# Values of two cross-attentions in seven block products instead of eight, with the context's sums kept in space that later rows will fill

## The chip, the cores and the metric

The kernel runs on one core of a Trainium2 chip. A core has a matrix engine (TensorE, "PE" in the profile; its weight loads are listed apart as "PEld"), a vector engine (VectorE, "DVE"), an activation engine (ScalarE, "ACT"), a general engine (GpSimd, "POOL") and a queue that issues transfers (SyncE, "SP"). The metric is the device time of one execution in microseconds, the median of several runs.

## What is computed

The reference is a stack of four transformer layers over four batches of 256 rows of 256 numbers, in 32-bit floats. Layer 0 has two cross-attentions to the same context and an MLP; layers 1, 2 and 3 are other attention variants on narrow heads. The change touches only the two attentions of layer 0:

```python
def _cross_attention(q_in, kv_in, wq, bq, wk, bk, wv, bv, wo, bo, bias_k, bias_v):
    qh = (q_in @ wq + bq).reshape(b, q_len, H, K)
    kh = (kv_in @ wk + bk).reshape(b, t, H, K)
    vh = (kv_in @ wv + bv).reshape(b, t, H, K)
    # one learned key and value are appended, then
    weights = softmax(einsum('bqhk,bthk->bhqt', qh, kh) / sqrt(K))
    ctx = einsum('bhqt,bthk->bqhk', weights, vh).reshape(b, q_len, H * K)
    return ctx @ wo + bo
```

Here H is 16 heads of K = 128, kv_in is the context (4 x 256 rows of 256), and wq, wk, wv are 256 x 2048. Queries, keys and values are thus three products of a 1024 x 256 matrix by a 256 x 2048 one, twice.

## The kernel before, in words

Layer 0 loops over two attentions (li), four head groups of four heads (hg) and two pairs of batches (bp): 16 rounds. In each round the queries, keys and values of 4 heads and 512 rows are made, then for each batch of the pair the scores, the softmax, the transposed weights, the weighted values and the projection by wo.

**Seven products for queries and keys.** A product of two matrices of 2 x 2 blocks takes eight block products; Strassen's method in Winograd's form takes seven, at the cost of sums of blocks. The routine seven (line 1029) does this. Its blocks are a 128 x 128 piece of the weights (the stationary operand) and 256 columns of the input. It runs p = 0 and 1 side by side, so it issues 14 products of 256 columns in four tasks on PE, each after the one before: first, second, third, fourth. Between them one PSUM bank, v[0], goes on being added to, while VectorE or ScalarE save its state into a tile u of a ring of three (UU, line 936), and VectorE forms the totals from PSUM and u into the output. The sums of weight blocks are made by GpSimd (sums, line 1015, four subtractions or additions for each head group) and lie in space that the MLP's weights will fill later (place["sq"], place["sk"] in mlp_w0); the sums of inputs are made by VectorE or GpSimd (differences, line 994). The first round's keys are made the plain way.

**Eight products for the values.** In each round the list tV (line 1212) has four tasks on PE. Each multiplies 128 rows of the context (stationary) with 512 columns of wv, in two accumulating products of 128x512; VectorE then adds the bias row bvb into the tile V. bvb is bv less the learned value's bias, and GpSimd subtracts that once for each head group.

**Rows.** rowbc (line 90) holds 3136 numbers of bias and scale rows for all layers, spread to all partitions by one load (all_rows, line 1120, issued as t_rows at line 1148). Layer 0 uses the first 768; the others belong to layers 1 to 3.

**What sets the order.** Nothing is ordered by hand. Each piece is a Task (line 171): an amount of PE time, tasks it must come after, tasks it must be planned behind without waiting for their data, ring buffers it takes and gives back (PSUM banks in the ring PS, V, E, u and so on), and Posts, the work of other engines that follows, each with its cost on every engine that may do it. plan (line 1533) runs a greedy simulation at build time: among the products that can start with least idle time of PE, within 0.2 us (SLACK, line 1524), it takes the one with the highest level, which is the length of the longest chain behind it, corrected by HANDICAPS (line 1648) for each stage and batch. A post goes to the engine that would end it first. Instructions are then issued in that order, and every engine keeps it (Pinned, line 124); the chip's semaphores make them wait for real. A task added anywhere can therefore move later choices.

**What stands around the change.** Weights of a head group live in the ring W0 of two sets (line 917) and are loaded when the group before last is done. t_f0 (line 1408) loads the MLP's weights into mlp_w0 once all queries and keys are made. opened (line 1454) frees layer 0's memory, once its last projections are planned, opens that of the later layers, and only then their weights are loaded. weighted (line 1349) reads V. All instructions carry line 132 in the profile, the helper that records them, so they are told apart by their tiles: wv, wk, wq are weights, ctxT the context, HT the normed input, craw and e the input differences of queries and keys (raw and the first EE tile), f the weight sums, u the saved states, V, qT, kT the results, and ps_pj, ps_s, ps_et, ps_o PSUM banks.

Of the kernel before, what the change touches and what calls it, by code (L numbers as in the profile page):

```python
# [51 lines left out]
def kernel(ctx: ExitStack, tc: tile.TileContext, a: dict, out: bass.AP):  # L52
# [861 lines left out]
    def l0_ring(n, shape, tag):  # L914
        return Ring([l0.tile(shape, F32, tag=f"{tag}{i}", name=f"{tag}{i}") for i in range(n)])
# [5 lines left out]
                for k, shape in (  # L921
                    ("wv", [P, 2, 512]), ("wq", [P, 2, 512]), ("wk", [P, 2, 512]), ("wo", [P, HG, D]),
                    ("bvb", [P, 512]), ("bvl", [P, 512]),
                )
# [5 lines left out]
    for place, f in zip(W0.tiles, mlp_w0):  # L930
        f = f.rearrange("p a b -> p (a b)")
        place["sq"] = f[:, :768].rearrange("p (n q c) -> p n q c", n=3, q=2)
        place["sk"] = f[:, 768:1536].rearrange("p (n q c) -> p n q c", n=3, q=2)
    V0, QT, KT = l0_ring(2, [P, 4, 512], "V"), l0_ring(2, [P, HG, 512], "qT"), l0_ring(2, [P, HG, 2, S + 1], "kT")
    E0, ET, CT = l0_ring(4, [P, HG, S + 1], "E"), l0_ring(3, [P, 2, S], "eT"), l0_ring(2, [P, HG, S], "cT")
# [72 lines left out]
    for bp in range(2):  # L1008
        def block(k, j, bp=bp):
            return ctxT[:, k, (2 * bp + j) * S : (2 * bp + j + 1) * S]  # L1010
# [17 lines left out]

    def seven(b, after, w, key, block, T, to, bias):


        v, u = {}, {}

        def A(p, i, k):
            return w["w"][2]["w" + key][:, k, (2 * p + i) * P : (2 * p + i + 1) * P]

        def sum_(n, p):
            return w["w"][2]["s" + key][:, n, p, :]

# [8 lines left out]

        def saved(n, of, i, gives=()):

            if not bias:
                return [copied(lambda: flat(n), lambda: v[of][2], 512, gives)]
            return [
                affine(
                    lambda p=p: flat(n)[:, p * S : (p + 1) * S], lambda p=p: v[of][2][:, p * S : (p + 1) * S], None,
                    lambda p=p: bias(p, i), gives if p else (),
                )
                for p in range(2)
            ]
# [13 lines left out]
        def second():  # L1073
            for p in range(2):
                product(0, p, sum_(0, p), T[:, 1, :])

        def third():
            for p in range(2):
                product(0, p, A(p, 1, 0), T[:, 0, :])
            for p in range(2):  # L1080
                product(2, p, sum_(1, p), T[:, 2, :], True)

        def fourth():
            for p in range(2):
                product(0, p, sum_(2, p), block(1, 1))
            for p in range(2):
                product(2, p, A(p, 1, 1), T[:, 3, :])

        def last(gives):

            if not bias:
                dst = lambda: to(0)[:, :, 1, :]
                return [copied(dst, lambda: pairs(0), 512, gives)]
# [9 lines left out]
            b, "full", 1.73, first, after, takes=[(PS, v, 0), (PS, v, 1), (UU, u, 0)],  # L1103
            posts=saved(0, 0, 0) + [total(0, 0, 1, 0, [(PS, v, 1), (UU, u, 0)])],
        )
        t2 = Task(b, "full", 0.86, second, [t1], takes=[(UU, u, 1)], posts=saved(1, 0, 1))
        t3 = Task(
            b, "full", 1.73, third, [t2], takes=[(PS, v, 2), (UU, u, 2)],
            posts=saved(2, 0, 1) + [total(1, 1, 2, 2, [(UU, u, 2)])],
        )  # L1110
# [3 lines left out]
        )  # L1114
        made = {}
        for p in range(2):
            made.update({(2 * p, 0): t1, (2 * p + 1, 1): t3, (2 * p, 1): t4, (2 * p + 1, 0): t4})
        return made

    def all_rows(e):  # L1120
        dma.dma_start(rowbc, a["rowvec"].to_broadcast([P, _RB_LEN]))

    finals = [[first_x], [first_x], [second["x"]], [second["x"]]]
    all_qk, all_l0, loads, last_grab, last_e, last_h, t_rows = [], [], [], [], [], [], None
    freed_w, freed_u, freed_e = [], [], []
    for li in range(2):
# [6 lines left out]
        for bp in range(2):  # L1133
# [4 lines left out]
            for b in (2 * bp, 2 * bp + 1):  # L1138
# [8 lines left out]
                if t_rows is None:  # L1147
                    t_rows = load(0, [], "rows", all_rows, 1568, behind=[tn])
                t_plus[b] = plus_row_to(b, [tn, t_rows], lambda b=b: Xb(b), f"L0_xattn_bo{li + 1}")
# [12 lines left out]
        for hg in range(NG):  # L1162
# [36 lines left out]
            for bp in range(2):  # L1199
# [11 lines left out]
                last_grab = [grab]  # L1211
                tV = []
                for i in range(4):
                    v = {}

                    def products(i=i, u=u, v=v, w=w, bp=bp):
                        at_ = (4 * bp + i) * P
                        for k in range(2):
                            pe(v["pt"][2], ctxT[:, k, at_ : at_ + P], w["w"][2]["wv"][:, k, :], k == 0, k == 1)

                    def add(e, i=i, u=u, v=v, w=w):
                        ve.tensor_tensor(u["V"][2][:, i, :], v["pt"][2], w["w"][2]["bvb"], ALU.add)

                    tV.append(
                        Task(
                            b0, "full", 1.71, products, [grab, t_w["wv"], t_w["bv"], t_ctx[b0 + i // 2]],
                            takes=[(PS, v, "pt")], posts=[Post(("DVE",), 605, add, gives=[(PS, v, "pt")])],
                        )
                    )
                made = [{}, {}]  # L1230
                if li == 0 and hg == 0 and bp == 0:
# [25 lines left out]
                for n, key in ((1, "k"), (0, "q")):  # L1257
# [8 lines left out]
                    def bias(p, i, h0=hg * HG, li=li):  # L1266
                        return bqs[li][:, h0 + 2 * p + i : h0 + 2 * p + i + 1]

                    done = seven(
                        b0, [grab, t_S[n], (t_Tq if key == "q" else t_Tk)[bp]], w, key,  # L1270
                        (blocks_q if key == "q" else blocks_k)[bp], (Tq if key == "q" else Tk)(bp), to,
                        bias if key == "q" else None,
                    )
                    made[n].update(done)
                tQ, tK = list(dict.fromkeys(made[0].values())), list(dict.fromkeys(made[1].values()))
# [3 lines left out]
                for bb in range(2):  # L1279
# [46 lines left out]
                    for h in range(HG):  # L1326
# [22 lines left out]
                        def weighted(h=h, x=x, y=y, u=u, bb=bb):  # L1349
                            for kc in range(2):  # L1350
# [6 lines left out]
                            Task(  # L1357
                                b, "full", 0.87, weighted, [t, tV[2 * bb], tV[2 * bb + 1]], behind=tC[:1],
                                takes=[(PS, x, "pt")] + ([(CT, c, "c")] if h == 0 else []),
# [47 lines left out]

    t_f0 = load(0, [t_cols[2]], "f0", run, 2048, (), all_qk)

# [43 lines left out]

    opened = Task(0, None, 0, None, behind=all_l0, posts=[Post(("POOL",), 1500, open_late)])
    opened.fills = [(r, len(r.tiles), len(r.tiles) + n) for r, n, _, _ in later] + [(r, 0, 2) for r in SHIFTS]
# [10 lines left out]
    def run(e):  # L1466
# [8 lines left out]
    t_L = {  # L1475
        k: Task(0, None, 0, None, [opened], posts=[Post(("POOL",), 3500, lambda e, k=k: layers[k].fill())], lag=2.0)
        for k in (1, 2, 3)
# [249 lines left out]
```

## Time and profile before

| What | us |
|---|---|
| median of 3 runs (1383.52 to 1384.44) | 1384.36 |
| the profiled execution | 1383.26 |
| its span, from the first to the last instruction | 1381.5 |
| PE busy within the span | 1333.6 |
| VectorE busy | 783.4 |
| ScalarE busy | 711.1 |
| GpSimd busy | 167.3 |
| last product with wv starts | 695.7 |
| first product of the MLP starts | 728.30 |

The profile is of one execution, so a sum of its rows is made against 1383.26 us; 1.76 us of that lie around the span. An engine's busy time says how much of the span it worked, not whether anyone waited for it. Groups are written out<-in, with partitions x elements; on PE, the part before the shape is rows x columns of the stationary operand. Products overlap in the array, so the distance between the starts of two neighbours says more about their cost than their lengths. Each product of 32-bit floats leaves two records.

### The profile page before, as it was taken

To read this page: it belongs to the slowest core of one execution; us is meant where nothing else is said; L and a number is where in the kernel's file an instruction comes from. 1 tells how busy PE (TensorE), PEld (TensorE's weight loads), DVE (VectorE), ACT (ScalarE), POOL (GpSimd) and SP (SyncE) were. 2 spreads that over 40 slices of the span, in tenths; PEclk is the share of its full clock that TensorE was granted. 3 is DMA by queue.
4 is the path that set the end of the run, shared out by engine and by line. 5 is a ranking of instruction groups with operands and counts; after the bars stand their busy time and mean duration, and the time that the engine had idled before them with its cause. 6 is when DMAs were issued, how large, how long until landed. Compare 5 with 4: busy or idle time off the path is not lost.

```text
span 1381.5 us, 21985 instructions
## 1 busy us (share of the span) xinstructions
PE 1333.6 (97%) x8343; PEld 1009.8 (73%) x8343; DVE 783.4 (57%) x2246; ACT 711.1 (51%) x1728; POOL 167.3 (12%) x283
## 2 busy tenths in 40 slices
PE   5999999999999999999999999999999999999996
PEld 3777787778878787787888867666565667776664
DVE  5655663556656546365542568572665443648886
ACT  2544344454444444344444335527545565889895
POOL 6102020002020200100003411101110002000000
PEclk9999999999999999999999999999999999999999
DMA  7000010100200101000004110000000000000000
GB/s 262 1 32 31 31 47 16 40 22 2 76 16 16 46 31 46 16 32 0 31 1 142 33 47 3 9 1 4 2 5 1 1 2 1 2 9 17 9 4 14
DMA packets 25482, 37.99 MB, mean 27 GB/s; under 512 B 2228, under 2 KB 16070, under 8 KB 25248
## 3 DMA queue, kind: packets, MB, share of 16 engines
q1 hardware_dynamic: 24496, 35.56, 7.9%
q0 software_dynamic: 608, 0.76, 0.5%
q8 instruction: 66, 1.08, 0.3%
q14 instruction: 40, 0.33, 0.1%
q10 hardware_dynamic: 272, 0.26, 0.1%
HBM read 35.52 MB, written 1.05 MB: 26 GB/s over the span
## 4 chain that ended last, share of the span: by engine, by line
PE 87%; DVE 7%; ACT 4%; DMA 1%; issue 1%; POOL 0%; SPq 0%; DVEq 0%; ACTq 0%
PE ps_et L132 24%; PE ps_s L132 22%; PE ps_pj L132 21%; PE ps_o L132 20%; DVE shift L132 2%; ACT eq L132 2%; DVE qk L132 1%; ACT qk L132 1%; DVE eq L132 1%; DMA wv<-in_L_xattn_wv_dram 1%; DVE X L132 0%; ACT e L132 0%; DMA wk<-in_L_xattn_wk_dram 0%; DVE u L132 0%; DVE craw L132 0%
## 5 line engine op out<-in xcount | busy, mean ns | idle before, releaser
L132 ACT ACTIVATE eq<-eq,nm 128x256 f32<-128x256 f32 x256 | 106.2, 509 | 0.0
L132 DVE TENSOR_SCALAR E<-E,rinv 128x257 f32<-128x257 f32 x256 | 84.2, 394 | 2.2
L132 PE MATMUL ps_o<-qk 32*128 32x256 f32 (+1 forms) x318 | 84.9, 459 | 0.3 <-ACT qk L132 0.3
L132 POOL TENSOR_TENSOR X<-X,rowbc 128x256 f32<-128x256 f32 x56 | 41.7, 767 | 340.1 <-DVE e L132 90.3
L132 PE MATMUL ps_et<-qk 32*128 32x256 f32 (+1 forms) x278 | 74.7, 450 | 0.2 <-DVE shift L132 0.2
L132 PE MATMUL ps_s<-qk 32*128 32x256 f32 (+1 forms) x232 | 69.8, 450 | 0.0
L132 PE MATMUL ps_pj<-qk 32*128 32x256 f32 (+1 forms) x196 | 67.1, 487 | 1.0 <-DVE shift L132 1.0
L132 POOL COPY kT<-lks 128x4 f32<-128x4 f32 x32 | 7.2, 236 | 427.5 <-PE ps_o L132 180.7
L132 DVE TENSOR_TENSOR X<-ps_et,X 128x512 f32<-128x512 f32 (+1 forms) x23 | 13.8, 599 | 69.5 <-PE ps_et L132 68.1
L132 PE MATMUL ps_pj<-eq,qk 32*128 32x256 f32 x196 | 50.5, 411 | 1.8 <-DVE qk L132 1.5
L132 PE MATMUL ps_o<-eq,qk 32*128 32x256 f32 x232 | 50.1, 411 | 0.1
L132 DVE TENSOR_REDUCE shift<-ps_o 128x1 f32<-128x512 f32 (+1 forms) x60 | 40.4, 684 | 16.4 <-PE ps_s L132 10.2
L132 PE MATMUL ps_et<-wo,cT 128*128 128x256 f32 x208 | 47.0, 379 | 0.0
L132 PE MATMUL ps_s<-eq,qk 32*128 32x256 f32 x168 | 45.3, 410 | 0.9 <-ACT qk L132 0.9
L132 PEld LDWEIGHTS ps_o<-qk 32*128 32x128 f32 x318 | 39.6, 183 | 7.8 <-issue 2.8
L132 PE MATMUL ps_et<-eq,qk 32*128 32x256 f32 x172 | 43.7, 403 | 0.1
L132 PEld LDWEIGHTS ps_et<-wo,cT 128*128 128x128 f32 x208 | 39.3, 190 | 5.2
L132 DVE TENSOR_REDUCE nm<-ps_pj 128x1 f32<-128x257 f32 x66 | 27.3, 419 | 24.2 <-ACT cT L132 19.5
L132 DVE TENSOR_REDUCE nm<-ps_et 128x1 f32<-128x257 f32 x64 | 26.6, 420 | 24.1 <-ACT cT L132 21.7
L132 DVE TENSOR_TENSOR X<-ps_pj,X 128x256 f32<-128x256 f32 (+1 forms) x13 | 6.9, 527 | 58.2 <-PE ps_pj L132 58.2
L132 PEld LDWEIGHTS ps_et<-qk 32*128 32x128 f32 x278 | 34.6, 183 | 7.2 <-issue 5.2
L132 PE MATMUL ps_s<-eT,V 128*128 128x256 f32 x156 | 39.7, 382 | 0.0
(527 smaller groups left out, 3797.5 us busy)
## 6 DMA issues: line engine op xcount, KB each, us to landing
wk<-in_L_xattn_wk_dram SPq DMA_DIRECT2D x8, 512.0 KB, 3.6
wv<-in_L_xattn_wv_dram SPq DMA_DIRECT2D x8, 512.0 KB, 4.1
wq<-in_L_xattn_wq_dram SPq DMA_DIRECT2D x8, 512.0 KB, 5.3
wo<-in_L_xattn_wo_dram SPq DMA_DIRECT2D x8, 512.0 KB, 4.0
bvb<-in_bv_dram SPq DMA_DIRECT2D x8, 256.0 KB, 5.6
bvl<-in_cols_dram SPq DMA_DIRECT2D x8, 256.0 KB, 5.8
f<-in_L_xattn_w_fc_dram SPq DMA_DIRECT2D x2, 1024.0 KB, 5.1
f<-in_L_xattn_mlp_w_dram SPq DMA_DIRECT2D x2, 1024.0 KB, 5.1
```

Of the source, the lines that this page charges most:

```text
L132: return lambda *args, **more: tc.keep_in_program_order(f(*args, **more))
```

## The change

In every round but the first (li = 0, hg = 0, bp = 0) the values too are made by seven. The parts are:

- **seven** takes its blocks as functions. For values, the stationary blocks are pieces of the context (two halves i of rows, two of columns k, p is the batch of the pair), the moving blocks are 256 columns of wv, and the row bvb is added where the state is saved and at the last step (with_row, VectorE only).
- **Sums of the context** S1 to S4 are made once for each batch (context_sums, on VectorE or GpSimd, 128x128) and stay through both attentions in rowbc, from column 768 on, where the rows of later layers would lie.
- **Sums of wv** are made once for each head group (value_sums, GpSimd, 128x256). One overwrites a block of wv, two lie in the tail of mlp_w0, one in a new tile t4. In the first group they come behind the old value tasks, which read wv.
- **rowbc** is loaded in two parts: its first 768 columns early, the others (rows_of(first_rows, _RB_LEN), 1184 KB) behind all the values. t_f0 is behind all the values too, and opened and the later layers' preparation wait for the second part.
- **weighted** waits for those value tasks that made its heads' half (values_of), of both batches' rows at once.

```diff
-                    ("bvb", [P, 512]), ("bvl", [P, 512]),
+                    ("bvb", [P, 512]), ("bvl", [P, 512]), ("t4", [P, 256]),
...
+        place["tv"] = [f[:, 1536:1792], f[:, 1792:], place["t4"]]
...
-    def seven(b, after, w, key, block, T, to, bias):
+    def seven(b, after, A, sum_, block, T, to, bias, row=None):
...
+        def with_row(dst, of, j, gives=()):
+            def run(e):
+                r = row(j).rearrange("p (o c) -> p o c", o=1).to_broadcast([P, 2, 256])
+                ve.tensor_tensor(dst(), pairs(of), r, ALU.add)
+
+            return [Post(("DVE",), 605, run, gives=gives)]
+
-        def saved(n, of, i, gives=()):
+        def saved(n, of, i, j, gives=()):
+
+            if row:
+                return with_row(lambda: flat(n).rearrange("p (q s) -> p q s", q=2), of, j, gives)
...
         def last(gives):
+            if row:
+                return with_row(lambda: to(0)[:, :, 1, :], 0, 1, gives)
...
-    def all_rows(e):
-        dma.dma_start(rowbc, a["rowvec"].to_broadcast([P, _RB_LEN]))
+    first_rows = _RB["L1_xattn_v_b"][0]
+    SV = rowbc[:, first_rows : first_rows + B * 4 * P].rearrange("p (b n c) -> p b n c", b=B, n=4)
+
+    def rows_of(lo, hi):
+        return lambda e: dma.dma_start(rowbc[:, lo:hi], a["rowvec"][:, lo:hi].to_broadcast([P, hi - lo]))
+
+    def context_sums(b):
+        def run(e):
+            on = ve if e == "DVE" else ge
+
+            def A(i, k):
+                return ctxT[:, k, b * S + i * P : b * S + (i + 1) * P]
+
+            S1, S2, S3, S4 = (SV[:, b, n, :] for n in range(4))
+            on.tensor_tensor(S1, A(1, 0), A(1, 1), ALU.add)
+            on.tensor_tensor(S2, S1, A(0, 0), ALU.subtract)
+            on.tensor_tensor(S3, A(0, 0), A(1, 0), ALU.subtract)
+            on.tensor_tensor(S4, A(0, 1), S2, ALU.subtract)
+
+        return Task(b, None, 0, None, [t_ctx[b]], posts=[Post(("DVE", "POOL"), {"DVE": 840, "POOL": 1600}, run)])
+
+    t_SV = [context_sums(b) for b in range(B)]
+
+    def value_sums(after, behind, w):
+        def run(e):
+            def B_(k, j):
+                return w["w"][2]["wv"][:, k, j * 256 : (j + 1) * 256]
+
+            T2, T3, T4 = w["w"][2]["tv"]
+            ge.tensor_tensor(T3, B_(1, 1), B_(0, 1), ALU.subtract)
+            ge.tensor_tensor(B_(0, 1), B_(0, 1), B_(0, 0), ALU.subtract)
+            ge.tensor_tensor(T2, B_(1, 1), B_(0, 1), ALU.subtract)
+            ge.tensor_tensor(T4, B_(1, 0), T2, ALU.subtract)
+
+        return Task(0, None, 0, None, after, posts=[Post(("POOL",), 2900, run)], behind=behind)
...
-                    t_rows = load(0, [], "rows", all_rows, 1568, behind=[tn])
+                    t_rows = load(0, [], "rows", rows_of(0, first_rows), 384, behind=[tn])
...
+                if li == 0 and hg == 0 and bp == 0:
...
+                    values_of = [[tV[0:2], tV[0:2]], [tV[2:4], tV[2:4]]]
+                    t_TV = value_sums([t_w["wv"]], tV, w)
+                else:
+                    if bp == 0:
+                        t_TV = value_sums([t_w["wv"]], [], w)
...
+                    done = seven(
+                        b0, [grab, t_TV, t_w["bv"], t_SV[b0], t_SV[b0 + 1]], A, lambda n, p, b0=b0: SV[:, b0 + p, n, :],
+                        block, T, to, None, lambda j, w=w: w["w"][2]["bvb"][:, j * 256 : (j + 1) * 256],
                     )
+                    values_of = [[[done[0, j], done[1, j]] for j in range(2)]] * 2
+                    all_v += list(done.values())
...
-                                b, "full", 0.87, weighted, [t, tV[2 * bb], tV[2 * bb + 1]], behind=tC[:1],
+                                b, "full", 0.87, weighted, [t, *values_of[bb][h // 2]], behind=tC[:1],
...
-    t_f0 = load(0, [t_cols[2]], "f0", run, 2048, (), all_qk)
+    t_f0 = load(0, [t_cols[2]], "f0", run, 2048, (), all_qk + all_v)
+    t_rows = load(0, [], "rows", rows_of(first_rows, _RB_LEN), 1184, (), all_v)
...
-    opened = Task(0, None, 0, None, behind=all_l0, posts=[Post(("POOL",), 1500, open_late)])
+    opened = Task(0, None, 0, None, behind=all_l0 + [t_rows], posts=[Post(("POOL",), 1500, open_late)])
```

## The prediction, made before the result was known

> **What bounds the kernel.** I read the engines' busy time first, then stretches of the span, then what TensorE waits for, then single tasks in order of time.
>
> ```profile
> PE 1333.6 (97%) x8343; PEld 1009.8 (73%) x8343; DVE 783.4 (57%) x2246; ACT 711.1 (51%) x1728; POOL 167.3 (12%) x283
> PE 87%; DVE 7%; ACT 4%; DMA 1%; issue 1%; POOL 0%; SPq 0%; DVEq 0%; ACTq 0%
> ```
>
> The first line is the page's busy time, the second the chain that ended last. TensorE (PE) is busy 97% of the span and is 87% of the chain. An average over stages is not enough, so the second view is the busy time by stretch (columns: stretch, length, then busy time of PE, its weight loads, VectorE, ScalarE, GpSimd, each with its count, then granted clock, DMA share, GB/s).
>
> ```profile
> 16.60:60.00 43.40, 40.74 (x160) 27.23 (x160) 31.52 (x84) 21.18 (x63) 21.55 (x32) 1.00 0.27 96
> 100.00:730.00 630.00, 627.45 (x2908) 505.88 (x2907) 340.00 (x849) 279.15 (x803) 59.39 (x101) 1.00 0.09 28
> 730.00:1381.50 651.50, 621.97 (x5089) 441.89 (x5088) 383.83 (x1245) 392.26 (x816) 77.45 (x130) 0.98 0.06 16
> 1200.00:1381.50 181.50, 163.16 (x1572) 115.52 (x1564) 132.82 (x602) 151.57 (x355) 1.42 (x2) 0.98 0.03 10
> ```
>
> The two first attentions, which alone the change touches, end near 728. From 100 to 730 PE idles 630.00 - 627.45 = 2.55 us (0.4%), while VectorE is busy 54% and ScalarE 44%: work taken off PE there is time taken off the span. After 730 PE idles 651.50 - 621.97 = 29.5 us, 18.3 of them in the last 181.5 us. Third view, all that PE waits for between 100 and 730 (total us, times, longest):
>
> ```profile
> PE ps_s L132 <- DVE u L132: 0.7, 3, 0.2
> PE ps_o L132 <- DVE u L132: 0.7, 3, 0.2
> PE ps_pj L132 <- DVE u L132: 0.7, 3, 0.2
> PE ps_et L132 <- ACT eT L132: 0.2, 1, 0.2
> PE ps_et L132 <- DVE u L132: 0.2, 1, 0.2
> ```
>
> Nearly all of it is the u tiles: the queries and keys, already made in seven products, and their handovers.
>
> **What is removed and added on TensorE.** Two kinds of tasks in order of time (start, length, instructions merged):
>
> ```profile
> 85.32 1.03 PE L132 MATMUL ps_et<-ctxT,wk 128*128 128x256 f32 x4
> 86.18 1.03 PE L132 MATMUL ps_s<-craw,f 128*128 128x256 f32 x4
> 87.05 1.03 PE L132 MATMUL ps_o<-e,f 128*128 128x256 f32 x4
> 88.29 1.13 PE L132 MATMUL ps_s<-craw,wq 128*128 128x256 f32 x4 [0.22 <-DVE u L132]
> ...
> 120.88 1.88 PE L132 MATMUL ps_s<-wv,ctxT 128*128 128x512 f32 x4
> 122.60 1.88 PE L132 MATMUL ps_pj<-wv,ctxT 128*128 128x512 f32 x4
> 124.32 1.88 PE L132 MATMUL ps_et<-wv,ctxT 128*128 128x512 f32 x4
> ```
>
> A product of the program leaves two records (the wv groups count 256, and the code has 2 layers x 4 head groups x 2 pairs x 4 tasks x 2 = 128 products). Lengths overlap, so I take the distance between starts: a value task (2 products of 512 columns) costs 1.72 us, two products of 256 columns 0.865 us.
>
> - Before, one pair of batches needs 4 tasks: 4 x 1.72 = 6.88 us.
> - After, 14 products of 256 columns: 7 x 0.865 = 6.06 us.
> - Saved: 0.82 us. Of 2 x 4 x 2 = 16 pairs the very first keeps the old form: 15 x 0.82 = **12.4 us** off PE, and 15 x 4 = 60 PE records fewer.
>
> The weight loads don't undo this: one took 190 ns and overlaps, and 256-column products, which need one load per 256 columns just as the new ones will, keep the 0.216 us per record.
>
> The Trainium skill (TensorE: Matmul & The Clock Gate, section Back-to-back issue gap) speaks against the change: for streams of load and matmul it gives 131 ns at 512 columns and 81 ns at 128, so narrow products are dearer per column. An estimate from it, read off the straight line at 256 columns (98 ns), would be 28 x 98 - 16 x 131 ns = 0.65 us more per pair, 9.7 us in all, and the change would lose. This trace's steps for fp32, 0.43 us and 0.216 us per record, are proportional to the columns, and they decide.
>
> **What is added on VectorE.** A value add out of PSUM (V<-ps,bvb, 128x512) takes 692 ns. Four per pair become seven (three saved with the row, three totals, one last), all allowed on VectorE alone: 3 x 0.69 = 2.1 us a pair, 31 us in all, on an engine with 290 us free between 100 and 730. They cost nothing as work; PE's products hide them. What is new is that PE waits for some: a seven is a chain of four tasks through one PSUM bank, with three handovers in which VectorE must have read the bank before PE adds to it again; 45 handovers. Queued behind a waiting product is all of PE. Lower bound 0, where other tasks fit between. Upper bound from the value rows: the task at 120.88 gives way at 122.60, its add ends at 122.80 + 0.69, so 0.89 us each and 40 us in all, if nothing else were ready. The nearest row is the same routine for queries and keys: 31 sevens, 93 handovers, and 11 waits of 0.22 us (10 above, one at 88.29). Their two sevens run beside each other and the value seven comes alone, so I take twice that share of waits, one handover in five: 9 x 0.22 = **+2.0 us**.
>
> The ring of three u tiles now serves three sevens of a pair, where it served two. Each holds one u from its second task to its fourth; with three so held none could go on, so some seven will be put off. PE then takes scores, turns or projections of the two pairs in flight; that is inside the bound above. If that cover is gone, at L0's end, values come late: in the old order they stand at 688.75 to 696, and the first mlp product only at 728.30.
>
> **GpSimd.** Eight value sums of four subtractions, 128x256: by the wk sums 0.73 to 0.85 us, 3.2 us each, 26 us in all, on an engine busy 59 of 630 us. In its queue, which keeps order, stand the q and k sums, bvb and the row adds behind them; weights come a head group ahead (wv issued at 100.65, used at 120.88), some 20 us for 11 us of work. For the first group the sums overwrite wv and wait for the last old value product (35.47 + 1.72); behind them in the queue stand the key differences that ran at 45.61, so 37.2 + 3.2 = 40.4 is early enough. The sums also slow VectorE:
>
> ```profile
> 506.13 1.14 DVE L132 TENSOR_SCALAR E<-E,rinv 128x257 f32<-128x257 f32 x4
> 200.13 2.62 DVE L132 TENSOR_SCALAR E<-E,rinv 128x257 f32<-128x257 f32 x4
> ```
>
> Four quotients took 1.14 us with GpSimd idle and 2.62 us while it made sums. One such group per new sum is 8 x 1.48 = 12 us of VectorE time, beside free VectorE time: 0 on PE, at worst the 0.2 to 0.3 us by which weight loads already wait for E now and then, some 2 us in all.
>
> The Trainium skill (SBUF — State Buffer, section Who interferes with whom) states that of a VectorE operation in a two-port mode and a GpSimd operation the later is fully blocked. By it each quotient could wait out a whole 0.73 us subtraction, 8 x 4 x 0.73 = 23 us of VectorE; the traced group shows half of that.
>
> **Sums of the context.** Four batches, four operations of 128x128 on VectorE or GpSimd. No such row exists; on VectorE the 128x256 form takes 0.41 us and 128x2 0.15, so 0.6 to 1.6 us a batch, I take 1.0. The first two fall beside PE's first keys (16.59 to 25.59), which hide them. The other two fall into 28 to 46, where VectorE runs without a gap and PE waited 1.51 us for xn at 34.86 and 0.97 for qT at 53.08. Nothing excludes a small gain, as the rows' first load shrinks from 1568 to 384 KB (it landed 11.9 us after issue, then POOL's row adds began). Range -1 to +3.2, taken **+1.0 us**.
>
> **Loads moved.** The rest of rowbc (1184 KB) is issued on SP after the last value product, behind the first mlp weights, whose load now also waits for the values. Its second half was issued at 683 and lands in 5.1 us; after the last values near 700 it lands near 706, then the rows in some 12 us, near 718, ahead of the first use at 728.30 and of the w1 loads, issued at 728.60. Cost 0; if late, PE would wait for the overrun, a few us at worst.
>
> **The sum.** -12.4 + 2.0 + 1.0 = -9.4 us. The profiled execution took 1383.26 us (span 1381.5 and 1.76 around it), so 1373.9 there; the median of the runs is 1.1 above it, so **1375.0**. With terms at their favourable ends, -13.4, hence 1371; with the idle after 730 also a tenth better, 1368.
>
> **Rivals.**
> - *Handovers eat the gain.* Values alone in their chain, on VectorE only: if each of 45 handovers costs 0.22 us or a little more, 9.9 us, the sum is -12.4 + 9.9 + 1.0 = -1.5, so 1382.9, no change. For: the wait exists 11 times already. Against: 82 of 93 handovers cost nothing. 0.11.
> - *The order after the two attentions gets worse.* The whole order is planned at once, with the same handicaps, and other arrival times change later choices. Price: PE idles 18.3 us after 1200, where ScalarE is busy 84%; if the batches arrive there bunched and that idle doubles, the sum is -9.4 + 18.3, so 1393.3. It decides from 9.4 + 2.8 = 12.2 us of added idle. For: that stage is short of PE work. Against: the later levels don't change. 0.12.
> - *The products don't get cheaper.* If 14 narrow products cost what 8 wide ones do, 1384.36 + 3 = 1387.4. The 0.865 us steps exclude nearly all of this; 0.02 in the slower share covers that and the far bound of the handovers (-12.4 + 40 + 3.2, so 1415), which needs that 45 times nothing else is ready.
>
> The forecast, 6 to 14 us faster, has 0.68, and 0.07 goes to a gain of 3 to 6 us by partly paid handovers. 0.2% is 2.8 us, about what a measurement of this kernel tells from no change. Faster: 0.68 + 0.07 = 0.75. Same 0.11. Slower 0.14. The range 1368 to 1385 leaves out the slower cases and little else; the likeliest case's own is 1370 to 1378.
>
> **What would show it.** PE records near 8283, PE busy near 1321. Idle of PE between 100 and 730 under 7 us, its new part put down to V or u. Value adds of about 0.69 us, 109 in number with all their forms. GpSimd busy near 193 us or more. The two attentions end near 719 instead of 728. Wrong would be: idle in that stretch above 12 us (handovers or the ring of u), idle after 730 above 40 us (the order), or a step of the new products above 0.9 us for two.

## The result, and the profile after

| | us |
|---|---|
| the kernel before, median of 6 runs (1381.44 to 1384.44) | 1383.88 |
| the changed kernel, median of 6 runs (1374.77 to 1378.16) | 1376.89 |
| difference of the medians | -7.0 |
| ratio, 95% interval | 0.9951 [0.9938, 0.9963] |
| profiled execution: before, after | 1383.26, 1378.02 |
| its span: before, after | 1381.5, 1376.2 |

The change makes the kernel faster, by 7.0 us instead of the 9.4 us forecast. The two profiled executions differ by less, 5.2 us: the changed kernel's is the second longest of its six. The busy time and the chain of the changed kernel's page:

```profile
PE 1325.0 (96%) x8523; PEld 1047.0 (76%) x8523; DVE 828.4 (60%) x2306; ACT 712.8 (52%) x1729; POOL 186.8 (14%) x315
PE 87%; DVE 7%; ACT 4%; issue 1%; DMA 1%; POOL 0%; SPq 0%; DVEq 0%; ACTq 0%
```

TensorE is still the bound. Its busy time fell by 8.6 us, not by the 12.4 us of the saved work. Busy time by stretch, with the columns of the prediction's table:

```profile
16.60:60.00 43.40, 38.85 (x132) 25.73 (x133) 36.21 (x82) 14.55 (x40) 26.28 (x43) 0.92 0.20 67
100.00:720.00 620.00, 617.31 (x3080) 538.62 (x3079) 373.19 (x887) 282.21 (x810) 72.85 (x115) 1.00 0.09 28
730.00:1376.20 646.20, 616.77 (x5061) 437.29 (x5060) 382.68 (x1237) 389.42 (x809) 74.57 (x122) 0.98 0.05 13
```

And all that TensorE waits for between 100 and 720:

```profile
PE ps_s L132 <- DVE u L132: 1.6, 7, 0.3
PE ps_pj L132 <- DVE u L132: 0.7, 3, 0.3
PE ps_o L132 <- DVE u L132: 0.2, 1, 0.2
```

In the middle nothing got worse: TensorE idles 620.00 - 617.31 = 2.69 us there (2.55 before), and its waits for u are 2.5 us in all (2.3 before), though 45 handovers were added. After 730 it idles 646.20 - 616.77 = 29.4 us (29.5 before). The loss stands in the first line: between 16.6 and 60 us TensorE did 132 records' work instead of 160, at a granted clock of 0.92 instead of 1.00.

As a mark for the end of the two attentions I take the moment when the first weights of layer 1 are issued, which come once layer 0's last projection is planned: 728.60 before, 722.56 after, so 6.0 us earlier, not 12.4. What follows takes 652.9 us before and 653.6 after. So some 6.3 us are lost ahead of the mark, and by the lines above ahead of 100 us.

**Where the first 60 us go.** The first norm (the scaling of the input rows) on VectorE, before the change, and then TensorE's first products that wait for it (start, length, what is done, idle time before it):

```profile
12.53 0.55 DVE L132 TENSOR_TENSOR ih<-mv 128x2 f32<-128x2 f32 x1
...
14.13 1.51 DVE L132 TENSOR_SCALAR xn<-X,mv 128x256 f32<-128x256 f32 x2
```

```profile
14.89 0.47 PE L132 MATMUL ps_s<-ident,xn 128*128 128x128 f32 x1 [7.28 <-DVE xn L132]
```

The same places in the changed kernel:

```profile
12.52 0.66 DVE L132 TENSOR_TENSOR rowbc<-ctxT 128x128 f32<-128x128 f32 x1
13.22 0.77 DVE L132 TENSOR_TENSOR rowbc<-rowbc,ctxT 128x128 f32<-128x128 f32 x1
13.91 0.28 DVE L132 TENSOR_TENSOR rowbc<-ctxT 128x128 f32<-128x128 f32 x1
14.11 0.81 DVE L132 TENSOR_TENSOR rowbc<-ctxT,rowbc 128x128 f32<-128x128 f32 x1
14.84 0.15 DVE L132 TENSOR_TENSOR ih<-mv 128x2 f32<-128x2 f32 x1
...
16.25 0.90 DVE L132 TENSOR_SCALAR xn<-X,mv 128x256 f32<-128x256 f32 x2
```

```profile
16.74 1.37 PE L132 MATMUL ps_s<-ident,xn 128*128 128x128 f32 x4 [8.98 <-DVE xn L132]
```

The first batch's context sums (rowbc<-ctxT) stand in VectorE's queue ahead of the norm, for 2.3 us, and TensorE gets its first normed rows 1.85 us later. (The second batch's sums ran on GpSimd, from 15.54 to 17.5 us, the other two on VectorE at 43.70 and 47.75.) Three of the four took 0.66 to 0.81 us, while GpSimd made weight sums; with GpSimd idle, at 48 us, the same operations took 0.28 to 0.29 us.

The second norm that TensorE waits for, before the change: VectorE's operations, then TensorE's wait.

```profile
33.52 0.15 DVE L132 TENSOR_TENSOR ih<-mv 128x2 f32<-128x2 f32 x1
33.70 0.16 DVE L132 TENSOR_TENSOR ih<-ih,mv 128x2 f32<-128x2 f32 x1
33.89 0.17 DVE L132 TENSOR_SCALAR ih<-ih 128x2 f32<-128x2 f32 x1
34.10 0.16 DVE L132 TENSOR_TENSOR mv<-mv,ih 128x2 f32<-128x2 f32 x1
34.30 0.73 DVE L132 TENSOR_SCALAR xn<-X,mv 128x256 f32<-128x256 f32 x2
```

```profile
34.86 0.78 PE L132 MATMUL ps_o<-ident,xn 128*128 128x128 f32 x4 [1.51 <-DVE xn L132]
```

The same in the changed kernel, with what GpSimd does beside it:

```profile
34.82 0.14 DVE L132 TENSOR_TENSOR ih<-mv 128x2 f32<-128x2 f32 x1
35.00 0.60 DVE L132 TENSOR_TENSOR ih<-ih,mv 128x2 f32<-128x2 f32 x1
35.63 0.66 DVE L132 TENSOR_SCALAR ih<-ih 128x2 f32<-128x2 f32 x1
36.32 0.64 DVE L132 TENSOR_TENSOR mv<-mv,ih 128x2 f32<-128x2 f32 x1
37.00 1.58 DVE L132 TENSOR_SCALAR xn<-X,mv 128x256 f32<-128x256 f32 x2
```

```profile
34.11 2.83 POOL L132 TENSOR_TENSOR X<-X,rowbc 128x256 f32<-128x256 f32 x4
36.90 0.73 POOL L132 TENSOR_TENSOR f<-wv 128x256 f32<-128x256 f32 x1
```

```profile
37.92 0.44 PE L132 MATMUL ps_o<-ident,xn 128*128 128x128 f32 x1 [2.58 <-DVE xn L132]
```

The chain takes 3.8 us instead of 1.5. GpSimd's queue is 4.9 us late: the second batch's context sums and the value sums of the second head group (23.58 to 26.7 us) stand ahead in it, so that the row additions (X<-X,rowbc) that began at 29.24 before, and were done ahead of this norm, begin at 34.11, beside it. The value sums of the first head group follow, from 36.90 to 40.0. An operation on two numbers a row takes 0.14 to 0.20 us by itself; beside GpSimd some took 0.55 to 0.74 us, others no longer than alone. TensorE waits 2.58 us at the end of that chain, and what it then does runs at a lowered clock:

```profile
36.50:37.50 1.00, 0.00 (x0) 0.00 (x0) 0.96 (x2) 0.00 (x0) 1.00 (x2) 1.00 0.00 0
37.50:38.50 1.00, 0.44 (x1) 0.18 (x1) 1.00 (x3) 0.00 (x0) 0.85 (x2) 0.56 0.00 0
38.50:40.00 1.50, 1.37 (x7) 1.37 (x8) 1.46 (x4) 0.43 (x1) 1.41 (x2) 0.50 0.00 0
40.00:42.00 2.00, 2.00 (x7) 1.49 (x6) 1.79 (x4) 0.78 (x3) 2.00 (x4) 0.50 0.01 4
```

The value behind the five busy times is the granted clock: it halves at the end of the gap, until 44.4 us. I count the loss as length x (1 - clock) over stretches of 5 us: 3.4 us for this one.

**The account of the profiled executions.** Work -12.4; idle time in the first 80 us +3.3 (18.83 against 15.56); lowered clock there +3.4 (none shown before); lowered clock after 730 +0.9 (12.20 against 11.35, up to the span's end); the first keys, which ran slower in the execution before, -0.9. The sum is -5.7; the spans differ by -5.3. The first keys, before and after:

```profile
16.39 5.78 PE L132 MATMUL ps_et<-ctxT,wk 128*128 128x512 f32 x8
17.90 4.92 PE L132 MATMUL ps_et<-ctxT,wk 128*128 128x512 f32 x8
```

The last section shows that this difference too is one of the clock.

### The profile page after: what moved, and what is told of

Its sections match the earlier page's. It is cut to its first block, busy times and chain, and to the rows that moved or that the text cites. A ratio compares the mean times of both kernels' runs of the same rounds, so it can differ in the third digit from the quotient of the medians.

```text
span 1376.2 us, 22438 instructions
## 1 busy us (share of the span) xinstructions
PE 1325.0 (96%) x8523; PEld 1047.0 (76%) x8523; DVE 828.4 (60%) x2306; ACT 712.8 (52%) x1729; POOL 186.8 (14%) x315
## 4 chain that ended last, share of the span: by engine, by line
PE 87%; DVE 7%; ACT 4%; issue 1%; DMA 1%; POOL 0%; SPq 0%; DVEq 0%; ACTq 0%
PE ps_s L132 25%; PE ps_et L132 22%; PE ps_o L132 21%; PE ps_pj L132 20%; ACT eq L132 2%; DVE shift L132 1%; DVE qk L132 1%; ACT qk L132 1%; DVE eq L132 1%; DMA X<-in_x_dram 1%; DVE X L132 0%; DVE u L132 0%; DVE ih L132 0%; DVE mv L132 0%; ACT e L132 0%
## 5 line engine op out<-in xcount | busy, mean ns | idle before, releaser
L132 PE MATMUL ps_pj<-qk 32*128 32x256 f32 (+1 forms) x298 | 92.2, 466 | 1.0 <-DVE shift L132 1.0
L132 PE MATMUL ps_o<-qk 32*128 32x256 f32 (+1 forms) x238 | 73.1, 454 | 0.4 <-ACT qk L132 0.4
L132 DVE TENSOR_TENSOR X<-ps_s,X 128x256 f32<-128x256 f32 (+1 forms) x25 | 13.6, 542 | 68.3 <-PE ps_s L132 65.7
L132 DVE TENSOR_REDUCE shift<-ps_pj 128x1 f32<-128x512 f32 (+1 forms) x62 | 42.0, 686 | 10.8 <-PE ps_et L132 5.0
L132 ACT ACTIVATE E<-ps_pj,nm 128x257 f32<-128x257 f32 x70 | 33.3, 478 | 29.1 <-DVE nm L132 29.1
L132 PEld LDWEIGHTS ps_pj<-qk 32*128 32x128 f32 x298 | 41.5, 183 | 8.1 <-DVE shift L132 3.1
L132 PE MATMUL ps_o<-kT,qT 128*128 128x257 f32 x144 | 42.2, 380 | 0.0
L132 DVE TENSOR_REDUCE shift<-ps_et 128x1 f32<-128x512 f32 (+1 forms) x52 | 35.3, 686 | 11.0 <-PE ps_s L132 4.4
L132 PE MATMUL ps_pj<-kT,qT 128*128 128x257 f32 x140 | 40.5, 381 | 0.7 <-DVE qT L132 0.7
L132 DVE TENSOR_REDUCE nm<-ps_o 128x1 f32<-128x257 f32 x72 | 29.9, 420 | 17.8 <-ACT cT L132 11.3
```

The costliest lines, as they stand in the source:

```text
L132: return lambda *args, **more: tc.keep_in_program_order(f(*args, **more))
```

## The experiments

Three theories. **START**: the new sums disturb the first 60 us, where VectorE and GpSimd are the bound, and that takes back what is missing. **HANDOVER** (the prediction's first rival): the values' seven has TensorE wait for its row additions. **ORDER**: the order after the two attentions got worse. The table has each profiled execution's end of the two attentions, TensorE's idle time and clock loss in the first 80 us, and what is lost against 728.60 less 0.82 us a round; times are medians against the kernel before on the same chip.

| kernel | rounds of seven | attentions end | idle, clock loss to 80 | lost | time against before | ratio, 95% |
|---|---|---|---|---|---|---|
| before | 0 | 728.60 | 15.6, 0 | 0 | 0 | |
| changed | 15 | 722.56 | 18.8, 3.4 | 6.3 | -7.0 | 0.9951 [0.9938, 0.9963] |
| e12, the same again | 15 | 722.4 | 19.3, 1.8 | 6.1 | -7.5 | 0.995 [0.9936, 0.9965] |
| e1 | 15 | 722.62 | 19.5, 3.4 | 6.3 | -4.4 | 0.997 [0.9959, 0.9982] |
| e3 | 15 | 723.85 | 19.6, 5.1 | 7.6 | -3.2 | 0.9972 [0.9961, 0.9983] |
| e5 | 8 | 723.50 | 16.6, 1.7 | 1.5 | -4.9 | 0.9966 [0.9952, 0.9979] |
| e6 | 14 | 723.62 | 19.6, 3.4 | 6.5 | -5.5 | 0.9967 [0.9955, 0.998] |
| e4 | 0 | 732.7 | 19.0, 1.7 | 4.1 | +3.8 | 1.0027 [1.0016, 1.0037] |
| e7 | 14 | 720.3 | 17.1, 1.7 | 3.2 | -9.9 | 0.9937 [0.9924, 0.995] |
| e8 | 15 | 722.3 | 18.6, 3.4 | 6.0 | -8.7 | 0.9941 [0.9929, 0.9953] |
| e9 | 14 | 720.1 | 18.0, 3.4 | 3.0 | -10.2 | 0.993 [0.9916, 0.9944] |
| e11 | 15 | 720.4 | 16.5, 3.4 | 4.1 | -9.3 | 0.9934 [0.9919, 0.995] |
| e10 | 14 | 718.7 | 16.7, 1.7 | 1.6 | -12.0 | 0.9913 [0.99, 0.9926] |

The column "lost" can be had in another way: idle time and clock loss, less the 15.6 us of before, agree with it within 1.6 us in every row but e9 (2.8).

### First attempts: the sums later, or fewer of them

**e1, the context's sums planned later.**

```diff
-    t_SV = [context_sums(b) for b in range(B)]
...
+        if li == 0:
+            t_SV = [context_sums(b, t_Tq) for b in range(B)]
```

> The changed kernel with one edit: the four context_sums tasks are planned behind the input differences of both pairs, so VectorE no longer makes the first batch's sums (12.52 to 14.92) ahead of the first norm. Theory START (what the change lost of its 12.4 us, some 6 us, is lost in the first 60 us): the first transposes of xn start near 14.9 instead of 16.74, and PE's idle before 20 falls by 1.8 us; the value block still stands ahead of the second norm's transposes, so the rest stays. Time 1374 to 1375.5. Rival HANDOVER (the loss is in the value chains, some 0.4 us per round): 1376.9, unchanged. Rival ORDER (any new order scatters the time by several us, whatever happens at the start): no relation between the start and the time, 1371 to 1381.

The first normed rows came back to their old time, but the end of the attentions didn't move (722.62): what was won at 15 us was lost at the second norm and after (waits of 2.46, 1.41 and 1.45 us). START's fix, as I had put it, missed. An unchanged end is also what HANDOVER had; e9 decides on that theory.

**e3, the value sums of the first two head groups later too** (value_sums planned behind t_Tq as well).

> As the run before, and the value_sums of the first two head groups are planned behind the input differences too, so GpSimd makes no sums of wv (23.58 to 26.7 and 36.90 to 40.0) while VectorE makes the second norm. START: VectorE's small operations of that norm are shorter, PE's 2.6 us wait for xn at 37.92 shrinks, and PE's clock falls for a shorter time; 1372.5 to 1374.5. HANDOVER: 1376.9. ORDER: 1371 to 1381 without relation to the start.

No better: 723.85, and 3.2 us below before where START had 9 to 11. The context's sums stood on VectorE from 46 to 50 us now, and TensorE waited 2.68 us at 52.77 for the queries behind them. They had only been moved to another place.

**e5, seven products in the second attention only** (the old value tasks in all of li = 0, the context's sums behind the last of them).

> Values by seven products only in the second attention (8 rounds); the first attention has the old value tasks, and the context's sums are planned behind its last ones. The start is issued in the order of the kernel before. START: 8 x 0.82 = 6.6 us less and no loss, 1377.3; PE busy to 60 us is 44.4 as in the kernel before. HANDOVER: 7.0 us of gain over 15 rounds is 0.47 us a round, so 8 rounds give 3.7 us, 1380.2. ORDER: 1372 to 1382.

The start keeps before's order of instructions, and only 1.5 us are lost; 8 x 0.82 = 6.6 less that is the 5.1 us found. The 1.5 us can be read from rows: the wait for the second norm was 2.45 us instead of 1.51 (+0.9), half a clock stood behind it (+1.7), and the first keys took 4.68 us instead of 5.78 (-1.1), which is why TensorE came early to that norm. So the 0.82 us a round are there: with these rows the 8 rounds gave 5.1 + 1.5 us. The time by itself doesn't decide: -4.9 us lies between START's -6.6 and HANDOVER's -3.7.

**e6, the first head group plain for both pairs**, the context's sums and the next value sums behind t_Tq.

```diff
-                if li == 0 and hg == 0 and bp == 0:
+                if li == 0 and hg == 0:
```

> The first head group of the first attention keeps the old value tasks for both pairs, the context's sums are planned behind the input differences, and the other 14 rounds use seven products. The start is issued in the order of the kernel before. START: 14 x 0.82 = 11.5 us less than the kernel before with at most 1 us lost to the moved sums, 1372.4 to 1373.4, so faster than the changed kernel by 3.5 to 4.5 us although PE has 0.8 us more to do; PE busy to 60 us near 44.4, granted clock 1.00 there. HANDOVER: 14 x 0.47 = 6.6 us of gain, 1377.3. ORDER: 1371 to 1381 without relation to the start.

VectorE's order was before's until 49.67 us; then all 16 context sums stood there in one block until 55.0 us, ahead of the softmax's maxima. TensorE idled 5.44 us ahead of 55.99, and the clock was halved from 54.6 to 61.5 us. 6.5 us lost again, at a third place, and 5.5 us below before where START had 10.5 to 11.5 and HANDOVER 6.6. In the changed kernel, e3 and e6 the sums cost at three places, each time with TensorE waiting behind VectorE's queue.

### The second set: take VectorE out of it

**e4, the context's sums alone on the kernel before** (and the split row load); nothing uses the sums.

> The kernel before, with only the context's sums (their 16 operations, planned on VectorE or GpSimd as in the changed kernel) and the split row load; the sums are used by nobody, the values stay in eight products. START (what is lost of the gain is lost in the first 60 us, because the sums stand ahead of the first norms): slower than before by 1.5 to 3.5 us, and layer 0 ends that much behind 728.60. Rival SECOND TASKS (the loss comes from the value sums and from the order of the first value tasks, not from the context's sums): within 0.7 us of before. The prediction's term was +1.0.

3.8 us slower, a little more than START's 1.5 to 3.5, and far from the rival's 0.7. TensorE's first normed rows came after a wait of 9.28 us instead of 7.28, the second after 2.86 instead of 1.51, with a half clock behind it. What follows the mark took 652.1 us against 652.9, so no cost of the split load shows. The prediction's term for this was +1.0 with a range up to +3.2.

**e7, e6 with the sums on GpSimd alone.**

```diff
-        return Task(..., posts=[Post(("DVE", "POOL"), {"DVE": 840, "POOL": 1600}, run)], behind=behind)
+        return Task(..., posts=[Post(("POOL",), 1600, run)], behind=behind)
```

> The changed kernel with the first head group in eight products for both pairs (14 rounds of seven instead of 15), and the context's sums on GpSimd alone, planned behind the query differences, where GpSimd has its idle stretch from 52 us. VectorE's first 128 instructions are then those of before. START: the start stays as before, so layer 0 ends 14 x 0.82 = 11.5 us before 728.60, near 717, and the time is 10 to 12 us below before. Rival WORK (a round saves less than 0.82 us in place, since TensorE's records are longer or its clock lower wherever there is more beside it): layer 0 ends near 722 to 724 as in every kernel so far, 5 to 7 us below before. Between the two: GpSimd's sums, now in one block near 58 to 68 us, stretch VectorE's maxima and give 2 to 4 us back.

9.9 us below before; by the mark (720.3) 3.2 us of the 11.5 are still missing, as the in-between case had it. The sums ran on GpSimd from 48.82 to 59.5 us, and this is what stands beside them in VectorE's and TensorE's rows:

```profile
51.79 2.02 DVE L132 TENSOR_SCALAR E<-E,rinv 128x257 f32<-128x257 f32 x4
53.73 0.68 DVE L132 TENSOR_TENSOR qT<-ps_o,u 128x512 f32<-128x512 f32 x1
```

```profile
54.46 2.00 PE L132 MATMUL ps_o<-ctxT,wk 128*128 128x256 f32 x4 [2.33 <-DVE qT L132]
56.25 1.89 PE L132 MATMUL ps_pj<-craw,f 128*128 128x256 f32 x4
57.96 1.04 PE L132 MATMUL ps_et<-e,f 128*128 128x256 f32 x4
```

The four quotients took 2.02 us (1.14 before), the queries' last addition came late, TensorE waited 2.33 us instead of 0.97, and its next two groups took twice their time.

**e8, the changed kernel with the context's sums on GpSimd, late** (15 rounds; the second pair of the first group in seven, as changed).

> The changed kernel with the context's sums on GpSimd alone, planned behind the query differences; the first pair of the first head group in eight products, its second pair in seven, as changed. If the context's sums on VectorE were the loss at the start: layer 0 ends near 717 to 718, 10 to 11 us below before. If the value sums of the first head group and the value tasks drawn ahead of the second norm are the loss (they stay here): layer 0 ends near 722 to 723, 6 to 7 us below before, as in the changed kernel.

With the context's sums out of VectorE's way, 6.0 us are still lost by the mark (722.3): the value sums ahead of 41 us and the value tasks drawn forward cost that by themselves. (The context's sums, on GpSimd from 42.7 to 51 us, cost little: TensorE was busy 37.27 of the 38 us from 42 to 80, and 36.88 before.) So the two causes hide each other: context sums alone 4.1, value part alone 6.0, both 6.3. In all three TensorE waits at the second norm: 2.86 us in e4, 2.67 and 1.95 in e8, 2.58 in the changed kernel. The time, 8.7 us below before, lies between the two cases; in the profiled execution what follows the mark took 649.2 us against 653.6, with 8.0 us of lowered clock against 12.2.

**e11, 15 rounds, all sums on GpSimd behind t_Tq** (e3 with the edit of e7).

> The changed kernel with its 15 rounds, but all sums on GpSimd behind the query differences: the context's and the value sums of the first two head groups. What stays is the planner's order, in which all four value tasks of the first pair are drawn ahead of the second norm. If that order costs the start: layer 0 ends near 722, as in the changed kernel. If it was the sums on GpSimd ahead of 41 us: near 718 to 720, as with the plain first group.

720.4, just above the second case: about 2 us of e8's loss were the value sums ahead of 41 us (the idle time to 80 us falls from 18.6 to 16.5), and 4.1 us stay. The planner still draws all four first value tasks ahead of the second norm (the sums that must follow them raise their level), and the norm's small operations still met work of GpSimd (input differences and row additions), at 0.63 to 0.68 us each. No run parts these two.

**e9, e7 with each row addition made twice.**

```diff
                 ve.tensor_tensor(dst(), pairs(of), r, ALU.add)
+                ve.tensor_tensor(dst(), pairs(of), r, ALU.add)
...
-            return [Post(("DVE",), 605, run, gives=gives)]
+            return [Post(("DVE",), 1300, run, gives=gives)]
```

> The kernel of the run with the plain first group and sums on GpSimd, with each addition of the row on the way from one product to the next made twice in a row on VectorE (the second writes the same numbers again; 98 more operations of about 0.69 us, the planner told of 1.3 us each). HANDOVER (each round waits for its additions): 3 of them stand in the path of each of 14 rounds, so about +29 us against that kernel. RING COVERS (other heads' work fills the wait): 0 to +4 us.

The count in that text is wrong: four, not seven, of a round's additions pass through this function, so 56 were added (84 into u instead of 42, 36 into V instead of 22). Three of the four stand in the path of each of 14 rounds, so HANDOVER's 29 us hold. Measured: 1372.35 against e7's 1372.64. TensorE's busy time between 100 and 717 us, in e7 and then in this kernel:

```profile
100.00:717.00 617.00, 614.41 (x3063) 535.58 (x3062) 370.75 (x881) 281.70 (x810) 73.49 (x118) 1.00 0.10 31
```

```profile
100.00:717.00 617.00, 614.54 (x3073) 537.22 (x3072) 402.35 (x925) 286.73 (x824) 73.85 (x118) 1.00 0.10 31
```

VectorE works 31.6 us more and TensorE idles 2.46 us instead of 2.59. HANDOVER falls: the longer handovers were covered, and RING COVERS holds.

**e10, the sums held back to where TensorE is full.** A copy of one column of the softmax weights stands ahead of the second head group's value sums on GpSimd, and the context's sums behind them; the sums overwrite the column.

```diff
+            if E:
+                ge.tensor_copy(T3[:, 0:1], E[1]["e"][2][:, 0, 0:1])
...
+                            t_TV = value_sums([t_w["wv"]] + first_tN, [], w, first_E)
+                            t_SV = [context_sums(b, [t_TV]) for b in range(B)]
```

> The kernel of the run with the plain first group and sums on GpSimd, but the value sums of the second head group and the context's sums are held back by a copy of one column of the softmax weights that VectorE finishes near 61 us, so that they run near 61 to 73 us, where TensorE was fully busy in every kernel and VectorE busy to a third. There the quotients of the first batches took 2.02 and 1.89 us beside the sums, and 1.14 us in the kernel before. START: TensorE's first 60 us are as in the kernel before (44.4 us busy, clock 1.00) and layer 0 ends 10.5 to 11.5 us before 728.60, at 717 to 718; the time is 9.5 to 12 us below before. Rival WORK: a later wait takes the place and layer 0 ends at 720 or later as with the sums at 49 to 59 us.

GpSimd's rows, and then the engines' busy time in this kernel:

```profile
49.44 0.90 POOL L132 TENSOR_TENSOR e<-ctxT,e 128x256 f32<-128x256 f32 x1
71.78 0.24 POOL L132 COPY f<-E 128x1 f32<-128x1 f32 x1 [21.44 <-DVE E L132]
72.09 0.73 POOL L132 TENSOR_TENSOR f<-wv 128x256 f32<-128x256 f32 x1
```

```profile
40.00:60.00 20.00, 18.67 (x94) 15.50 (x93) 15.69 (x42) 13.28 (x43) 3.19 (x4) 1.00 0.01 2
60.00:80.00 20.00, 20.00 (x104) 17.73 (x103) 9.71 (x21) 10.15 (x28) 7.67 (x16) 1.00 0.09 27
```

The column came at 71.8, not near 61, and did its work all the same: from 60 to 80 us TensorE is busy without a gap while GpSimd makes the sums. The kernel takes 1370.81 us, 12.0 below before; 14 x 0.82 = 11.5 lies within the interval (10.2 to 13.8). It has the lowest median of all versions. By the mark (718.7, forecast 717 to 718) 9.9 us are won and 1.6 still lost, and these are e5's: the same wait for the second norm (2.50 us, +1.0) and the half clock behind it (+1.7), less first keys of 4.61 us instead of 5.78 (-1.2), with TensorE's and VectorE's order of instructions as before to 75 us. So what is missing stands at a place that the sums don't touch; no cost of them shows where they stand.

**e12, the changed kernel again**, beside e10 and e11 on one chip.

> The changed kernel itself, unedited, on the same chip as the two others, for a direct comparison: 6 to 8 us below before; START puts the run with the held-back sums 3 to 5 us below this one.

1375.31 us, 7.5 below before and 4.5 above e10, as forecast. e10 does 0.8 us more of work on TensorE, so its place for the sums, with the plain first head group, is worth some 5 us.

## Why the prediction was right or wrong, step by step

- **The saved work, -12.4: right.** Two products of 256 columns with value operands start 0.86 to 0.87 us apart (104.99, 105.86, 106.72), and e5 and e10 show 0.82 us a round once their one late wait is counted in. The narrow products showed no price of their own.
- **Handovers, +2.0: too high; they cost nothing** (idle time 2.69 against 2.55 us, and e9). The rival built on them falls with them. Nor did the ring of u tiles add a wait of note: 2.5 us in all against 2.3.
- **Context sums, +1.0, range -1 to +3.2: the step that failed.** It said "the first two fall beside PE's first keys (16.59 to 25.59), which hide them". The first batch's stood at 12.52, ahead of the norm that those keys and their neighbours wait for, and so hid behind nothing. Alone they cost 3.8 us (ratio 1.0016 to 1.0037, so 2.2 to 5.1). The length was well estimated for an idle GpSimd (1.0 us a batch, against 0.6 to 1.6), not beside its sums (2.3 us); the place was not read off: the context's turned rows are in place at 12.5, and the norm's next operation starts at 12.53.
- **GpSimd's sums, "0 on PE, at worst ... some 2 us": right from 60 us on, wrong ahead of it.** The prediction had read the stretching of VectorE from rows at 200 and 506 us, where TensorE has cover, and looked at the first group's queue only for what comes late in GpSimd, not for the second norm on VectorE beside it, nor for the row additions that the sums push onto that norm. e8 prices this part at 6.0 us, for both the sums and the order that they bring; the two parts together cost 6.3.
- **Loads, 0: right.** The second part of the rows landed 5.7 us after issue (12 were forecast), and e4, which has the split, lost nothing behind the mark.
- **ORDER: it fell.** Idle time after 730 is 29.4 against 29.5 us, where 40 would have shown it.
- **The signs.** The attentions were to end near 719 and do at 722.56; e10 has 718.7. TensorE's busy time was to be 1321 and is 1325.0, with 3.4 us of half clock at the start in it. The 109 operations of 0.69 us that form the values are there. GpSimd is busy 186.8 us, not 193: the four operations of a value sum took 2.9 us rather than 3.2, and some of the key differences moved to VectorE, against one batch of the context's sums that GpSimd took. The record count was a slip: by two records a product, 14 products leave 28 against 16, so 12 more a round and 8343 + 180 = 8523, as found, not 8283.

The forecast's direction and range held because the term that it got right is the large one. The two errors at the small end had opposite signs: handovers 2.0 too dear, the start some 5 us too cheap. That the medians miss the forecast by only 2.4 us is luck in part: by the mark the miss is 3.4.

## What to carry to other kernels

A saving on the engine that bounds the middle of a kernel can be paid back at its start, where other engines are the bound: price each added operation at the place in its queue where it will stand, from the time its inputs are ready, and ask who waits behind it. Moving such work later on the same busy engine only moved the loss here; putting it on an idle engine and holding it back until the bound engine had cover took it away. And a short gap of TensorE can cost more than its length, because of the clock behind it.

## What the runs showed of the hardware

- **Short gaps halve TensorE's clock, in fixed windows.** The clock's entries in the 13 packed traces last whole multiples of 3.41 us (but for the last, which the end of the trace cuts): halved ones one or two (a loss of 1.7 or 3.4 us), full ones 5, 10 or 223 and the like. Between 30 and 60 us every gap of 2.06 us or more had a halved stretch at it or within 2 us behind it, and the gaps of 1.45 to 1.73 us that stood by themselves had none. Counted by these windows, each of the 14 falls there came right behind a window in which TensorE idled 1.90 us or more, and no window with 1.73 us or less was followed by one. Behind 730 us, where other products run, windows with as little as 0.34 us of idle time were, so idle time alone doesn't decide there. The Trainium skill (TensorE: Matmul & The Clock Gate, section Why this matters for your kernels) asks for no idle gaps over some 3 us; here less was enough. Its Part 1 gives windows of about 3.4 us that run on freely, with half clock as the idle state; the length of the stretches here agrees, and their place against the kernel's start differs from execution to execution.
- **A granted clock of 1.00 can mean that there is no entry.** The first entry of the clock comes 18.2 to 22.6 us into the span; ahead of it the views read 1.00. The second keys' eight records take 3.60 us in every execution. If the first keys ran at half speed until the first entry, they take 3.60 us plus half of the time from their start to it: before, 3.60 + (20.76 - 16.39) / 2 = 5.78; after, 3.60 + (20.54 - 17.90) / 2 = 4.92. Both are what was measured, and the other 11 executions agree within 0.02 us. So the first keys' -0.9 in the account, and the faster first keys of e5 and e10, come from where the clock's windows happened to fall.
- **The same lowered stretches make runs of one kernel differ.** Behind the attentions the kernels lost 6.0 to 13.8 us of clock, and took 648.2 to 653.8 us; the difference of the two lies between 638.7 and 642.2 in all. The 36 runs of the kernel before beside the experiments go from 1378.90 us at a mean clock of 0.994 to 1384.45 at 0.991. So a table row can move by 2 to 3 us for this alone: e1 and the changed kernel took 1377.09 and 1376.89 us, but the kernel before took 1381.53 beside the one and 1383.88 beside the other. That is why verdicts on single microseconds above go by the mark. Whether the kernels with GpSimd's sums have fewer such stretches by more than chance stays open.
- **VectorE slows beside GpSimd by more than the operation's size.** For two numbers a row 0.15 us became 0.55 to 0.74 in many places (in the changed kernel once 1.10, beside a 1.26 us operation of GpSimd), and stayed at 0.15 in others; 0.28 became 0.66 to 0.81 for 128x128, 1.14 became 2.02 for four quotients. The Trainium skill (SBUF — State Buffer, section Who interferes with whom) says that VectorE operations with two SBUF inputs contend with GpSimd's reads, and calls the ports that they share an exclusive lock. The half microsecond added even to the smallest operation would fit the rest of a 0.72 us subtraction; no run here shows that it is this.
